# A cross-attention kernel: the hand-written order of its first two batches drawn anew

## The chip, the cores and the metric

The kernel runs on one core of one Trainium2 chip. The metric is the device time of one execution in microseconds (us); less is better. Engines: PE (TensorE, matmuls; PEld is its weight load), DVE (VectorE), ACT (ScalarE), POOL (GpSimd) and SP (SyncE, which here only issues DMAs). "POOLq" and "SPq" are the queues in which POOL and SP issue DMAs. Each engine works through its own instructions in program order and waits, in place, for what an instruction needs.

## The reference

x is 32 batches of 512 rows by 640 columns, the context 32 batches of 77 rows by 1024 columns, all in float32. The context has 77 rows, which is the length of its text part, so the object, other and ip parts are empty; what is left to compute is one attention over 77 keys with 20 heads of 32 columns:

```python
q = _heads(hidden_states @ to_q_w)
h_txt = _sdpa(q, _heads(ehs_txt @ to_k_w), _heads(ehs_txt @ to_v_w))
out = _merge(h_txt)
out = out @ to_out_w + to_out_b
out = (out + residual) / RESCALE
```

The softmax runs over the 77 keys, the scale is 1/sqrt(32), the residual is x, RESCALE is 1.

## The kernel before

**Number format.** Each float32 operand is split into a high part (a copy rounded to fp32r) and a low part (the difference). A product is three matmuls: high by high, high by low, low by high. So each "step" of products below is three PE instructions, the high part of anything is a copy on ACT, and the low part is a subtraction on DVE or POOL.

**First stage: keys and values of the context.** The context of all batches is 2464 rows, worked in groups of 512, the fifth and last of 416. For each group the rows are transposed in eight chunks k (DVE, tile craw), split (tile ct, ACT and DVE), and multiplied by the key and the value weights, giving five column blocks j of 128 each. Keys are split (tile ks) and stored in k_dram; values are transposed (DVE, tile vs), split and stored in v_dram. This part, up to about 200 us, is not touched by the change: it covers the first groups, and the keys of the fourth.

**Second stage: attention.** Per batch there are five column blocks (four heads each). For one block n: queries (five steps over k, tile pq, one PSUM bank), high copy and low parts with copies across halves (tile qt); scores in four row tiles t (tile sc, three PSUM banks); a row maximum (DVE, nm); exponentials with their sums (ACT, tile pn, four instructions per row tile); a reciprocal (DVE, rs) and normalisation (POOL); a blockwise transpose (DVE, one tile z); four stores of z to DRAM (tile pd); and, four blocks later (LAG = 4), two loads back (tile raw), split into tile pp (ACT, DVE, POOL), six value passes (PE, tile pa, one buffer), the sum of two halves (ACT copy aw, two adds on DVE), and the split into tile at. When all five blocks of a batch are there, the output projection (tile po, with wo_s) adds up in steps, bias and residual are added (tile xr) and the rows stored. x of the next batch is loaded, transposed and split meanwhile (tiles xs, xt).

**The order.** Nothing is scheduled by the compiler: three tables of tokens are worked through one by one, and each token issues one small piece. FILL covers the end of the first stage together with batches 0 and 1; PLAN one batch, repeated for 29 batches; LAST_ the last batch. A token's place in the table sets the order on the engine that runs it, and the order of buffer allocations; between engines only data and buffers set the time.

**How a token is read.** "Y" tokens (function special) belong to the first stage or to set-up; j is a column block, k a chunk, i a quarter:
- YVjk: value products of the fourth group (PE); Ytj, Yhj, Ylj: its transpose (DVE), high (ACT) and low part (DVE); Ysji: its stores (SP).
- Yrk, Yfk, Ydk: transpose (DVE), high (ACT) and low part (DVE) of chunk k of the last group's context.
- YJjk: key products of the last group (PE); YIj, Yij, Yoj: high (ACT), low (DVE), store (SP).
- YCjk: value products of the last group (PE); YTj, YHj, YLj: transpose (DVE), high (ACT), low (DVE); YDji: stores (POOL's queue).
- Yzi, Yai, YUc, Yuc: x of batch 0, loaded (POOL's queue), transposed (DVE), high (ACT) and low part (POOL); Yxi: x of batch 1 loaded (SP).
- Yqk, YQ, Yg, Yc: the first block's queries; Yk: its keys loaded (SP); Ym, Yn, Yp: clearing of tiles (POOL); Ywj: output weights of block j loaded into wo_s (SP); Yb: bias.

Other tokens have a batch letter, a block and an operation (function issue): "a" is the batch of the table's start, "b" the one behind it, and a block number 0 to 4. So a3s0 is row tile 0 of the scores of batch 0, block 3. Operations: q queries of the next block, Q its high part (ACT), k copies across halves (POOL), g low parts (DVE); s scores (PE), m maximum (DVE), e exponentials (ACT); r, N, z reciprocal (DVE), normalisation (POOL) and transpose into z (DVE) of the block before; w its stores (SP); d loads of raw (SP); c casts into pp (ACT), l and R its low parts (POOL, DVE); v value passes (PE); A copy of the lower half (ACT), a adds of the halves (DVE); h and L high and low part of at for the block before (ACT, DVE); p projection steps (PE), f adds (DVE), o stores, b bias (POOL), ur residual loaded; T, X, x transposes, high and low parts of x (DVE, ACT, POOL), ux loads of x, uk and uv loads of keys and values (SP), K copies of keys (POOL).

Buffers that matter for the change: ct has 9 buffers, so a chunk of the last group takes the place of one whose five value products are done; vs has two (j even and odd), so a transpose waits for the stores of the one before it; z and pa have one each; b2L, for instance, is the last reader of the pa tile that b2v0 and b2v1 write again.

Of the kernel before, what the change touches and what calls it, by code (L numbers as in the profile page):

```python
# [51 lines left out]
def kernel(  # L52
# [732 lines left out]
    def low_query(n, w):  # L785
# [1 line left out]
        nc.vector.tensor_tensor(qt[rows, 1 + w, :], pqs[n][rows], qt[rows, 0, :].bitcast(F32), ALU.subtract)  # L787

    FILL = (
# [43 lines left out]
    ).split()  # L833

    PLAN = (
# [292 lines left out]
```

## Time and profile before

| | us |
|---|---|
| median of 3 runs | 1865.92 |
| lowest, highest | 1861.2, 1865.97 |
| the profiled execution | 1860.52 |
| its span, first to last instruction | 1858.7 |

The page gives busy times by engine, then views of stretches, of one engine's timeline and of waits. In a row of a timeline the columns are start and duration (us), engine, line of the code, operation, output<-input, shape, and the number of instructions merged into it; in square brackets stands the idle time of the engine just before, and what ended it. A row of a stretch has its bounds and length, then busy time and count of PE, PEld, DVE, ACT and POOL, the granted clock, and the DMA engines' share and GB/s. Line numbers: L204 key and value products of the context, L542 queries, L577 scores, L602 exponentials, L694 value passes, L750 projection, L171/L179/L183 the context's transpose and split, L256/L262/L266 the same for values, L588 maximum, L617 normalisation, L624 the transpose into z, L633 the stores of z, L712 the adds of halves, L726/L731 the split into at, L672 the low part of pp, L1037 the output weights.

### The profile page before, as it was taken

Reading aid. Unit: us, or ns where it says so; the run is one execution under the profiler, and the core shown is the slowest. Engines: PE = TensorE matmul, PEld = TensorE weight load, DVE = VectorE, ACT = ScalarE, POOL = GpSimd, SP = SyncE. Lnnn points to the kernel's source line nnn. Section 1 sums busy time; section 2 is a strip of 40 time slices with the busy share of each in tenths; the row PEclk is TensorE's granted clock in tenths of the full one; section 3 lists DMA queues with packets and bytes.
Section 4 is the critical chain, followed back from the end, with each engine's and each line's share of the span. In section 5 each row is a group of like instructions: output and inputs, shape, how many; then the busy total and the mean of one; then the engine's idle time right before and its main releaser. Section 6 shows DMA issues by size and latency. Waiting matters only on the chain.

```text
span 1858.7 us, 37494 instructions
## 1 busy us (share of the span) xinstructions
PE 1843.8 (99%) x10332; PEld 1656.9 (89%) x10332; DVE 1563.8 (84%) x2502; ACT 1524.9 (82%) x6218; POOL 1301.7 (70%) x1120
## 2 busy tenths in 40 slices
PE   9999999999999999999999999999999999999999
PEld 7888897889999999999999999999999999999998
DVE  5444458899999999999999999999999999999996
ACT  3232248999999999999999999999999999999984
POOL 1100158787887787777778777887788878877874
PEclk9999999999999999999999999999999999999999
DMA  9879779889898888989988989899899988888875
GB/s 186 197 196 251 179 189 261 248 244 243 238 243 242 238 239 227 246 236 232 247 236 240 240 239 242 234 236 245 231 236 247 242 239 240 232 236 240 237 219 192
DMA packets 563295, 431.37 MB, mean 232 GB/s; under 512 B 191120, under 2 KB 471120, under 8 KB 563088
## 3 DMA queue, kind: packets, MB, share of 16 engines
q1 hardware_dynamic: 558192, 413.16, 84.6%
q0 software_dynamic: 4800, 15.65, 2.6%
q8 instruction: 85, 1.39, 0.3%
q14 instruction: 122, 1.00, 0.2%
q10 hardware_dynamic: 96, 0.16, 0.0%
HBM read 247.17 MB, written 181.64 MB: 231 GB/s over the span
## 4 chain that ended last, share of the span: by engine, by line
PE 93%; ACT 2%; DMA 1%; DVE 1%; SPq 1%; issue 1%; POOL 0%; DVEq 0%; ACTq 0%; POOLq 0%
PE po L750 30%; PE pq L542 28%; PE pa L694 12%; PE sc L577 11%; PE pk L204 6%; PE pv L204 6%; ACT pn L602 1%; DMA pd<-z 1%; SPq L531 0%; SPq L633 0%; DVE z L624 0%; POOL xt L320 0%; DMA v_dram<-vs 0%; DVE pp L672 0%; DMA cs<-in_ctx_dram 0%
## 5 line engine op out<-in xcount | busy, mean ns | idle before, releaser
L602 ACT ACTIVATE pn<-sc,nm 128x77 f32<-128x77 f32 x2560 | 795.8, 342 | 39.5 <-DVE nm L588 33.1
L750 PE MATMUL po<-wo_s,at 128*128 128x320 f32 x3840 | 708.1, 311 | 0.1
L750 PEld LDWEIGHTS po<-wo_s,at 128*128 128x128 f32 x3840 | 620.1, 189 | 41.5 <-DVE xr L765 0.6
L542 PE MATMUL pq<-xt,wq_s 128*128 128x512 f32 x2400 | 597.5, 394 | 1.1 <-DVE qt L787 0.8
L602 ACT ACTIVATION_READ_ACCUMULATOR pn<-sc,nm 128x1 f32 x2560 | 567.2, 222 | 0.0
L542 PEld LDWEIGHTS pq<-xt,wq_s 128*128 128x128 f32 x2400 | 436.6, 188 | 80.9 <-ACT pn L602 1.2
L617 POOL TENSOR_TENSOR pn<-pn,rs 128x1232 f32<-128x1232 f32 x160 | 388.0, 2425 | 91.2 <-DVE rs L612 87.5
L694 PE MATMUL pa<-pp,vb 128*128 128x512 f32 x960 | 341.6, 404 | 3.7 <-DVE at L731 2.0
L577 PEld LDWEIGHTS sc<-kb,qt 128*128 128x128 f32 x1920 | 303.9, 188 | 16.6 <-ACT pn L602 2.3
L588 DVE TENSOR_REDUCE nm<-sc 128x4 f32<-128x308 f32 x640 | 295.2, 466 | 23.0 <-PE sc L577 18.9
L577 PE MATMUL sc<-kb,qt 128*128 128x154 f32 (+1 forms) x1920 | 302.7, 274 | 2.7 <-ACT pn L602 1.9
L783 POOL CAST qt<-qt 64x512 fp32r<-64x512 f32 x320 | 196.8, 615 | 142.2 <-ACT qt L779 127.3
L712 DVE TENSOR_TENSOR pa<-pa,aw 64x512 f32<-64x512 f32 x320 | 222.1, 694 | 50.1 <-ACT aw L708 42.7
L624 DVE STREAM_TRANSPOSE z<-pn 128x1280 f32<-128x1280 f32 x160 | 241.1, 1507 | 14.1 <-DMA pd<-z 8.1
L679 POOL TENSOR_TENSOR pp<-raw,pp 64x512 fp32r<-64x512 f32 x160 | 206.7, 1292 | 64.7 <-ACT pp L661 56.1
L708 ACT COPY aw<-pa 64x1024 f32<-64x1024 f32 x160 | 162.1, 1013 | 88.4 <-PE pa L694 87.5
L787 DVE TENSOR_TENSOR qt<-pq,qt 64x512 fp32r<-64x512 f32 x320 | 216.6, 677 | 6.0 <-ACT qt L779 1.1
L320 POOL TENSOR_TENSOR xt<-xs,xt 128x512 fp32r<-128x512 f32 x160 | 203.6, 1300 | 20.0 <-ACT xt L316 15.2
L743 POOL TENSOR_TENSOR xr<-xr,bias 128x640 f32<-128x640 f32 x128 | 202.6, 1584 | 14.2 <-DMA xr<-in_x_dram 3.9
L672 DVE TENSOR_TENSOR pp<-raw,pp 128x1024 fp32r<-128x1024 f32 x160 | 196.2, 1226 | 0.0
L694 PEld LDWEIGHTS pa<-pp,vb 128*128 128x128 f32 x960 | 174.0, 189 | 14.9 <-ACT pp L663 2.8
L663 ACT CAST pp<-raw 128x1024 fp32r<-128x1024 f32 x160 | 168.5, 1053 | 1.0 <-DMA raw<-pd 1.0
(46 smaller groups left out, 1584.8 us busy)
## 6 DMA issues: line engine op xcount, KB each, us to landing
pd<-z SPq DMA_DIRECT2D x640, 160.0 KB, 3.3
raw<-pd SPq DMA_DIRECT2D x160, 512.0 KB, 4.5
xr<-in_x_dram SPq DMA_DIRECT2D x128, 320.0 KB, 3.8
out_dram<-xr SPq DMA_DIRECT2D x127, 320.0 KB, 3.7
xs<-in_x_dram SPq DMA_DIRECT2D x124, 320.0 KB, 5.9
raw<-pd SPq DMA_DIRECT2D x160, 128.0 KB, 4.1
v_dram<-vs SPq DMA_DIRECT2D x80, 192.0 KB, 4.1
k_dram<-ks POOLq DMA_DIRECT2D x20, 512.0 KB, 4.3
```

Source lines behind the costliest of these rows:

```text
L204: nc.tensor.matmul(held[j][:, :gn], w[:, k, a, :], cts[g, k][:, c, :gn], start=(k == 0 and n == 0), stop=(k == NK - 1 and n == 2),)
L542: nc.tensor.matmul(pqs[n], wq_s[:, k, a, j * P : (j + 1) * P], xts[b, k][:, c, :], start=(k == 0 and m == 0), stop=(k == NC_ - 1 and m == 2),)
L577: nc.tensor.matmul(sc[:, cols], qt[:, m, t * P : (t + 1) * P], keys_, start=(m == 0), stop=(m == 2),)
L588: nc.vector.tensor_reduce(nm, sc[:, :KCOLS].rearrange("p (h k) -> p h k", k=NKEY), AX.X, ALU.max, negate=True)
L602: nc.scalar.activation(pnb[n % 2][:, at, :NKEY], sc[:, i * NKEY : (i + 1) * NKEY], AF.Exp, bias=nm[:, i : i + 1], accum_out=sms[n][:, at : ...
L617: nc.gpsimd.tensor_tensor(pf, pf, rs.unsqueeze(2).to_broadcast([P, NQ * HPC, NKEY]), ALU.mult)
L624: nc.vector.transpose(z.rearrange("p b t j -> p t b j"), pn.rearrange("p (t h) k -> p t (h k)", t=NQ).rearrange("p t (b i) -> p t b i", i=Q),)
L679: nc.gpsimd.tensor_tensor(pp[64:, 4, :], raw[:64, 2, :], pp[:64, 4, :].bitcast(F32), ALU.subtract)
L694: nc.tensor.matmul(pas[n][:, p, :], vb[:, p, t, :], pp[:, c, :], start=(c == p), stop=(c == p + 2),)
L712: nc.vector.tensor_tensor(pa[64 * p : 64 * p + 64, 0], pa[:64, p], aw[:, p], ALU.add)
L750: nc.tensor.matmul(pos[b, t, h][:, :HALF], ats[b * NC_ + j][:, a, t * P : (t + 1) * P], wos[0][:, j, c, h * HALF : (h + 1) * HALF], start= ...
L787: nc.vector.tensor_tensor(qt[rows, 1 + w, :], pqs[n][rows], qt[rows, 0, :].bitcast(F32), ALU.subtract)
```

## The change

Only the table FILL is changed. It has the same 809 tokens before and after, each once; 37 of them stand at the same place. PLAN and LAST_ and all functions stay. By groups:
- the value products of the fourth group (YV) come in another order: YV20 to YV22 and YV40 sooner, YV11 to YV13 and YV31 later;
- the first transposes on DVE: Yt0 is now ahead of Yr0, and the transposes of x (Ya) are ahead of Yr3 and Yr4;
- the last group's keys: block 0 and 1 are taken first (YJ00 to YJ07 within the first 13 key steps), blocks 3 and 4 later, so the last ones (YJ33 to YJ37, YJ43 to YJ47) stand behind the first value step of that group, YC00, and behind queries a0q0 to a0q2;
- loads of keys, values, x and output weights (Yk, uk, uv, ux, Yw) and the stores of z (w) stand in another order on SP;
- in batches 0 and 1, steps of DVE, ACT and POOL change places by some positions; YL2 goes from behind a4N to block 3, YL4 from ahead of b0m0 to behind b0r; b1z and b2z go ahead of b1a0 and b2a0; b2L goes behind b2R.

The core of the diff:

```diff
--- before.py
+++ after.py
@@ -787,49 +787,49 @@
     FILL = (
 ...
-        "YV00 YV10 YV20 YV11 YV30 YV31 YV01 YV12 YV02 YV13 YV32 YV03 YV04 YV05 YV14 Yr0 YV06 Yf0 Yz1 Yd0 "
-        "YV07 Yz2 YV15 Yt0 YV40 Yz0 Yr1 Yz3 YV21 Yr2 Yf1 YV41 Yh0 YV42 Yf2 YV33 Yd2 Yr3 YV22 Yl0 YV23 "
-        "Yf3 Yd1 Ys00 YV16 Yr4 Ys01 YV24 Ya1 Ys02 YV43 Ya2 YV34 Ys03 Yf4 Yd3 YV35 Yr5 Yd4 YV25 Ya3 YV17 "
-        "YV44 Yt1 YV26 Ya0 Yf5 YV36 YU0 YV27 Yh1 YV45 YU1 Yt2 YV46 YU2 Yd5 YU3 Yl1 YV37 Yu2 Yr6 Yh2 Ys11 "
-        "YV47 Yf6 Yl2 Ys13 Yu1 Yr7 Ys10 Yd6 Yf7 Ys21 Ys22 Ys23 Ys12 Yt3 Yd7 YU4 Yu4 Yu3 Yu0 Yx0 Ys20 Yx2 "
-        "Yx1 Yh3 Yn0 Yt4 YJ00 YJ01 YJ20 YJ21 YJ10 YJ02 YJ22 YJ30 YJ11 YJ03 YJ12 YJ13 YJ23 YJ14 YJ24 YJ15 "
-        "YJ04 YJ05 YJ06 YJ16 YJ25 YJ31 YJ07 YJ32 YI0 YJ17 Yi0 Yq0 Yl3 YI1 Yo0 Yh4 YJ26 Yi1 YJ40 Yl4 Yo1 "
 ...
-        "Yk011 YJ47 YI3 a0K00 YC00 Yi3 YI4 a0K01 a0q0 Yi4 Yo3 a0q1 Yo4 Yn1 YC01 Ys40 Ym0 a0s0 a0q2 Ys42 "
 ...
-        "a3uk030 a1K10 a2q4 a3uk011 YD11 YC20 a2w1 a2Q YD10 a2w2 YC21 a2e3 a2g1 a2w0 a1K11 YC22 a2k0 "
-        "a2w3 YC23 a3r a2g0 a3uk020 YC24 a3N a3uk001 YC25 a3uk010 YC26 YC27 a3q0 a2x1 a3q1 a3z a3X2 a3q2 "
-        "a2k1 a3X3 a3s0 a3x2 a3X4 a3q3 a3m0 YT2 a3d0 a3d1 a4d1 a3w1 a3w3 a3e0 a3s1 a3x3 a3q4 a3w0 a3m1 "
 ...
-        "YC33 a4c0 a3g1 a4v1 a3e2 a4v0 a3k1 a3s3 a4q0 a3m3 a4l a3e3 a4s0 a4s1 a4m0 YC34 b0d0 a4K00 YH2 "
-        "a4v2 a4r b0ux3 a4s2 a4e0 a4N YL2 a4v3 a4ux1 a4q1 a4q2 a4v5 a4s3 a4K01 a4v4 b0uk111 YC41 a4m1 "
 ...
-        "b0v1 YD33 b1T1 b0q2 YH4 b0s1 YL4 b0q3 b0m0 YD40 b2T3 b0e0 b0v0 b0q4 YD42 b0r b1T2 YD41 b0v2 b0Q "
 ...
-        "b1Q b1v0 Yw0 b1m2 b1e0 b1v3 b1v2 Yb b1g1 b1v5 b1v4 b1s3 b1k1 b1g0 b1A b1k0 b1m3 b2q0 b2d1 b2c1 "
-        "b1a1 b2x1 b2q1 b1a0 b2c0 b2q2 b1z b2h b2l b2s0 b1e3 b2q3 b2L b2q4 b1w1 b1e2 b2m0 b1w2 b2v1 b2R "
-        "b2v0 b1w3 b2s1 b2Q b2v2 b2uv00 b2v3 b2e0 b2m1 b2k1 b2v5 b1w0 b2r b3p0 b2g0 b2d0 b2N b2v4 b2s2 "
-        "b2g1 b2A b2uv05 b2s3 b3uk011 b2m2 b3q0 b3c0 b2uv01 b2m3 b2a0 b2e1 b3q1 b2uv02 b2k0 b2a1 b3q2 "
-        "b3d1 b1K10 b2e2 b2uv06 b2z b2b0 b3s0 b3uk031 b3q3 b3h b3q4 b3L b3l Yw3 b3c1 b3p1 b3m0 b2w1 b3p4 "
 ...
-        "b3g1 b2w2 b3v3 b3v5 b3uk001 b3N b3X2 b3s2 b3m1 b3uk010 b3p6 b3X3 b3m2 b4q0 Yw4 b3A b3uk020 b3p7 "
 ...
-        "b3uk030 b4s0 b4h b3p3 b4c1 b4l b4q4 b4L b3w2 b3e2 b4d0 b4m0 b4v1 b4R b4d1 b4Q b4p9 b3w1 b4e0 "
 ...
 ...
+        "YV00 YV10 YV20 YV21 YV22 YV01 YV23 YV30 YV40 YV02 YV41 YV03 YV24 YV04 YV11 Yz3 YV42 Yz1 YV05 "
+        "Yz0 YV06 Yz2 YV07 YV43 Yt0 YV25 Yr0 YV44 Yf0 YV26 Yd0 Yr1 YV12 Yf1 YV31 Yh0 YV13 Yl0 YV32 Yd1 "
+        "Ys02 Yr2 YV14 Ys01 Yf2 YV33 Ys00 Yd2 YV45 Ya1 Ys03 YV15 Yr3 YV46 Yr4 Yf3 Ya3 YV16 YV27 Ya0 YV34 "
 ...
+        "YU1 Yd5 YU2 Ys13 Yu1 Yf6 Yr7 Ys12 Yd6 Yf7 Ys22 YU3 Yu2 Yd7 YU4 Ys11 Yu4 Ys23 Ys20 Yu3 Yt3 Yx0 "
+        "Yn0 Yh3 Yt4 YJ00 YJ01 YJ02 YJ10 YJ11 YJ03 YJ20 YJ04 YJ12 YJ05 YJ21 YJ06 YJ07 YJ22 YJ30 YJ23 "
 ...
+        "YJ42 Yi2 YJ31 Yl4 Yo2 Yq1 Yx1 Yx3 Yq2 Yq3 YJ32 YJ43 Yk000 Yq4 Yk030 Yk010 YC00 YQ Yk021 YJ44 "
 ...
+        "Yk031 YJ36 Yk011 a2T3 a0q1 a0K01 Ys30 YJ37 a0K00 a2X0 Ys43 a0q2 YI3 YJ47 Yi3 a0q3 Yo3 YI4 a0q4 "
 ...
+        "a2q0 YH1 a2m1 a2uv07 a2q1 YL1 a2e1 a2s2 YD12 a2q2 a2m2 YD10 a2e2 a2s3 a2q3 YD11 a3uk030 a2m3 "
+        "a2z a3uk011 YC20 a2X1 a1K11 a3uk021 a2q4 YD13 a2e3 a3uk031 a2x1 YC21 a2w2 a2Q YC22 a2w1 a2e0 "
+        "YC23 a3uk000 a2g0 a2k0 YC24 a2w3 a2k1 a2w0 YC25 a3r a2g1 b1uv16 a3N YC26 a3uk020 YC27 a3s0 a3q0 "
 ...
+        "a3x3 a3q3 a3X4 a4d1 YC31 YH2 a3w0 a3x4 YC32 a4c0 YL2 a3w3 a3q4 a4c1 a4ux1 a3s2 a4K01 a3m1 YC40 "
 ...
+        "a4R YC35 a3e3 YD20 a4q0 b0d1 a4v2 a4v5 a4r a4v4 a4N a4s0 a4A a4s1 a4m0 a4q1 a4m1 b0c1 a4a0 a4s2 "
 ...
+        "b0m0 YH4 YD30 b0q2 b0m1 b0e0 b0r YL4 b0s2 b0N b2T3 b0q3 b1d0 b0e1 b0v1 b1T2 b1d1 b0v3 b0q4 b0T0 "
 ...
+        "b1v2 b1v5 Yw1 b1Q b1v4 b1s3 b2X1 b2uv01 b1g1 Yb b1A b1m3 b1g0 b1k1 b2c0 b1k0 b1a1 b1e3 b2q0 b2l "
+        "b1z b2c1 b2q1 b1a0 b1e2 b1w1 b2s0 b2uv00 b0uk110 b2h b2q2 b2m0 b1w2 b2R b2e0 b2s1 b1ur0 b2q3 "
+        "b1w0 b2r b0uk100 b2L b2q4 b2N b2uv03 b2m1 b2s2 b2Q b1w3 b2v1 b2m2 b2v0 b2e1 b2d0 b2v3 b2g1 b2v2 "
 ...
+        "b2k0 b3d0 b3X2 b3uk030 b2a1 b3q2 b2e3 b3x2 b2z b3q3 b3q4 b3X3 b1K10 b3X4 b2a0 b2b0 b2w0 b3s0 "
 ...
+        "b3s3 b3A b3uk020 b4q0 b3m3 b3x3 b2uv06 b4q1 Yw4 b3e3 b3a1 b3ur1 b4q2 b3a0 b3k1 b3uk001 b4q3 "
 ...
+        "b4v0 b4R b4v1 b4d0 b4p9 b3w3 b4p8 b4e0 b4v3 b3uk021 b4g0 b4b1 b4v2 b3w2 b4g1 b4s2 b4ux0 b4v4 "
 ...
     ).split()
```

46 rows, old and new, of the table FILL are left out of this document.

## The prediction

> **What bounds the kernel now.** I read first the page's busy shares, then the table of stretches, then TensorE's timeline for the places where it stands still, and last the rows of the engines that end those waits.
>
> ```profile
> span 1858.7 us, 37494 instructions
> PE 1843.8 (99%) x10332; PEld 1656.9 (89%) x10332; DVE 1563.8 (84%) x2502; ACT 1524.9 (82%) x6218; POOL 1301.7 (70%) x1120
> ```
>
> TensorE is busy 99% of the span, so only its idle time can be won, and only work that makes it idle can be lost.
>
> ```profile
> 200.00:250.00 50.00, 49.70 (x236) 43.58 (x235) 23.16 (x37) 13.24 (x25) 14.05 (x15) 1.00 0.72 186
> 250.00:300.00 50.00, 49.30 (x263) 45.24 (x262) 32.64 (x50) 32.94 (x156) 40.01 (x43) 1.00 0.82 198
> 300.00:350.00 50.00, 44.71 (x229) 37.12 (x229) 45.03 (x73) 45.91 (x198) 41.46 (x41) 1.00 0.88 262
> 350.00:392.00 42.00, 41.29 (x242) 37.16 (x241) 38.50 (x60) 38.40 (x165) 31.41 (x28) 1.00 0.90 251
> 392.00:441.00 49.00, 49.00 (x286) 44.61 (x285) 44.67 (x72) 45.06 (x191) 39.18 (x34) 1.00 0.89 241
> ```
>
> Columns are the stretch, then busy time of PE, PEld, DVE, ACT and POOL. FILL runs from 200 to about 355 us. TensorE idles 0.3 + 0.7 + 5.3 + 0.7 = 7.0 us up to 392, and not at all in the batch after it (49.00 of 49.00): from there on it is the bound, so a delay that FILL leaves stays in the end, one for one, and so does a gain. Here are the places:
>
> ```profile
> 228.09 14.24 PE L204 MATMUL pk<-ct,wk_s 128*128 128x416 f32 x75 [0.21 <-ACT xt L316]
> ...
> 286.29 0.34 PE L577 MATMUL sc<-kb,qt 128*128 128x154 f32 x1 [0.69 <-POOL qt L783]
> ...
> 312.77 0.73 PE L577 MATMUL sc<-kb,qt 128*128 128x308 f32 x3 [1.90 <-ACT pn L602]
> 318.25 0.47 PE L694 MATMUL pa<-pp,vb 128*128 128x512 f32 x1 [0.89 <-DVE at L731]
> 321.37 2.31 PE L542 MATMUL pq<-xt,wq_s 128*128 128x512 f32 x9 [0.81 <-DVE qt L787]
> 325.64 0.70 PE L694 MATMUL pa<-pp,vb 128*128 128x512 f32 x2 [0.20 <-DVE at L731]
> 341.26 0.73 PE L542 MATMUL pq<-xt,wq_s 128*128 128x512 f32 x2 [0.21 <-POOL xt L320]
> 344.66 0.47 PE L694 MATMUL pa<-pp,vb 128*128 128x512 f32 x1 [1.16 <-ACT pp L663]
> ```
>
> In order these are YJ00, a3s0, b1s0, b1v1, b2q0, b2v1, b4q3 and b4v1. Their waits add up to 6.1 us. Between 300 and 350 ACT (45.9 of 50) and VectorE (45.0) are nearly full, and the waits end on them.
>
> **The change, part by part.** The table holds the same 809 steps in another order, so no instruction is added or removed: every cost is a wait that goes, comes or changes place. The sum is made against the profiled execution's own 1860.5 us (span 1858.7 and 1.8 around it).
>
> *First part, to the last keys.* VectorE now starts with Yt0, and its transposes of x (Ya) stand ahead of Yr3 and Yr4. TensorE takes YJ07 after 12 other J steps instead of 22. By the row at 228.09 a step is 3 x 14.24/75 = 0.57 us, so it is reached at 228.1 + 12 x 0.57 = 234.9, about 5.7 us sooner.
>
> ```profile
> 222.10 1.57 DVE L306 STREAM_TRANSPOSE xs<-xs 128x640 f32<-128x640 f32 x2 [3.38 <-DMA xs<-in_x_dram]
> ...
> 227.86 0.55 DVE L183 TENSOR_TENSOR ct<-craw,ct 128x416 fp32r<-128x416 f32 x1
> 228.55 0.69 DVE L266 TENSOR_TENSOR vs<-vs 128x512 fp32r<-128x512 f32 x1
> 229.16 0.60 DVE L171 STREAM_TRANSPOSE craw<-cs 128x416 f32<-128x416 f32 x1
> ...
> 231.93 1.16 DVE L183 TENSOR_TENSOR ct<-craw,ct 128x416 fp32r<-128x416 f32 x1
> ```
>
> Yd7 must be done by then. Behind the landing of x (222.1) VectorE has four Ya (0.78), five Yr (0.55 to 0.60), five Yd (0.55), two Yt and two Yl (0.69 each as the upper row): 3.1 + 2.8 + 2.8 + 2.8 = 11.5 us, so Yd7 ends at 233.6 with no hindrance, and at 234.8 if the last two Yd take 1.16 us as the one at 231.93 did while POOL worked on xt. The cover is between 1.3 and 0.1 us; what is missing of it TensorE would lose at YJ06 and YJ07. I take +0.3 here, bounds -0.2 (YJ00's wait goes) and +1.8 (three slow ones). Drawing nine J steps behind YC00, and three query steps ahead of YJ47, costs TensorE nothing: it has other steps of the table in their place, and what is late next, YI3 and YI4, only feeds stores on SP.
>
> *Second part, batch 0.* The 0.69 us at a3s0 go: POOL did a3N and a2x1 ahead of a2k1, the copy that a3s0 needs.
>
> ```profile
> 284.28 1.29 POOL L320 TENSOR_TENSOR xt<-xs,xt 128x512 fp32r<-128x512 f32 x1
> 285.63 0.61 POOL L783 CAST qt<-qt 64x512 fp32r<-64x512 f32 x1
> ```
>
> In the new table a2k1 stands ahead of a3N. In exchange three query steps move behind a3s0, which is neutral. On SP a3uk030 to a3uk031 now come ahead of a2w2. They overwrite keys that a2s3 still reads, and the stores of a2 wait behind them; but a1w was issued sooner, and I find a2w ending where it ended before. I cost it at 0; without that cover it is the four issues, about 2 us by the rows of SP below, which a3z would feel.
>
> *Third part, where the time is.* ACT is full from b0e0 on, and b0e0 waited for VectorE:
>
> ```profile
> 308.51 0.33 ACT L602 ACTIVATE pn<-sc,nm 128x77 f32<-128x77 f32 x1 [1.11 <-DVE nm L588]
> ```
>
> ```profile
> 294.76 2.69 DVE L266 TENSOR_TENSOR vs<-vs 128x416 fp32r<-128x416 f32 x1 [0.17 <-ACT vs L262]
> ...
> 303.54 0.58 DVE L266 TENSOR_TENSOR vs<-vs 128x416 fp32r<-128x416 f32 x1
> ...
> 307.44 0.59 DVE L266 TENSOR_TENSOR vs<-vs 128x416 fp32r<-128x416 f32 x1
> ```
>
> Between a4m0 and b0m0 VectorE loses YL2 (2.69 us, moved ahead to a3) and YL4 (0.59, moved behind b0m0), 3.3 us. TensorE gives a4s0 about 1.4 us later (2.1 us of products more ahead of it, less the 0.69), and a4g1 will wait some 0.7 us for a4Q. So b0m0 comes 1.2 us sooner; bounds 0 and 1.9. That lead is spent again: up to b1g0 VectorE has YL4 (0.59) and b1m3 (0.46 by the row at 325.43 below) more to do, so b2q0, which needs b1g0, starts 0.15 us sooner. It is the point where the sum is taken anew, since VectorE and not TensorE sets it; b1s0's and b1v1's waits lie ahead of it and may change size freely (b1q0 to b1q2 now come ahead of b1s0, and wait for b0g0 instead).
>
> ```profile
> 322.08 1.42 DVE L712 TENSOR_TENSOR pa<-pa,aw 64x512 f32<-64x512 f32 x2 [0.48 <-ACT aw L708]
> 323.43 1.49 DVE L624 STREAM_TRANSPOSE z<-pn 128x1280 f32<-128x1280 f32 x1
> 324.85 0.64 DVE L731 TENSOR_TENSOR at<-pa,at 128x512 fp32r<-128x512 f32 x1
> 325.43 0.45 DVE L588 TENSOR_REDUCE nm<-sc 128x4 f32<-128x308 f32 x1
> 325.81 1.20 DVE L672 TENSOR_TENSOR pp<-raw,pp 128x1024 fp32r<-128x1024 f32 x1
> 326.94 0.46 DVE L588 TENSOR_REDUCE nm<-sc 128x4 f32<-128x308 f32 x1
> 327.33 0.23 DVE L612 RECIPROCAL rs<-sm 128x16 f32<-128x16 f32 x1
> ```
>
> These rows are b1a1 with b1a0, b1z, b2L, b2m0, b2R, b2m1, b2r. The only pa tile is free for b2v0 when b2L is done. The new order is b1a1, b1z, b1a0, b2m0, b2R, b2r, b2L: 0.45 + 1.20 + 0.23 = 1.9 us more ahead of b2L, which then ends near 327.3. TensorE has two score steps more ahead (0.7) and would be there at 326.1: it waits 1.2 instead of 0.20, that is +1.0. Behind it the 0.21 at b4q3 is covered, and at b4v1 TensorE comes 0.6 us later for its larger queue (b4s1, b4v0) and 0.6 for the delay, so that the 1.16 vanish nearly whole: -1.16 + 0.0. Sum from b2q0 on: -0.15 + 1.0 - 0.21 - 1.1 = -0.5.
>
> *Output weights.* Yw2, Yw0, Yw1 move within a few issues; Yw3 comes sooner. Yw4 has five other loads ahead of it on SP that it had not, and three fewer: two issues, about 1.0 us by the rows of SP below.
>
> ```profile
> 340.41 0.43 SPq L1037 DMA_DIRECT2D wo_s<-wo_dram x1
> ```
>
> It landed in time for b4p9, the step right behind b4v1. Bounds 0 (it still lands in time) and +1.4 (that 1.0 with the 0.43 of its own issue); I take +0.3, nearer to the first since b4p9 also comes later. **The sum:** -0.5 + 0.3 = -0.2 us; the +0.3 of the first part lies ahead of b2q0 and is inside its lead. So 1860.5 becomes 1860.3. The runs shown are 1861.2, 1865.92 and 1865.97, and with the profiled one that makes two near 1861 and two near 1866. I put the base in the middle of 1860.5 and the median, 1863.2, and predict 1863.0.
>
> **A rule against it.** The row at 294.76 is 2.1 us longer than its like at 303.54, and POOL's a4N ran beside it. The Trainium skill (SBUF — State Buffer, Who interferes with whom) says that a VectorE instruction with two SBUF inputs and a GpSimd instruction that reads SBUF lock each other out, whichever starts second waiting for the whole of the first. This trace agrees there. By that rule YL4, now between b0r and b2T3 just as b0r releases b0N, could be the one that waits, and the sum would be +1.9 instead of -0.2.
>
> **The rivals.**
>
> *YL4 is caught as YL2 was* (b0N wins by a hair): +2.1 us on VectorE ahead of b1g0, so b2q0 and all behind it: 1863.0 + 2.1 = 1865.1. Against it: YL4 is next in VectorE's own queue, and b0N must hear of b0r first.
>
> *x lands late.* Yr3 to Yd7 stand behind x now, where Yr3 and Yr4 were ahead. Each microsecond beyond 222.1 is lost at YJ03 to YJ07; 3 us gives 1866.
>
> *Slower: z holds VectorE.* One mechanism, at b1z, b2z and b3z: the transpose overwrites z, so it needs the four stores of the one before landed, and VectorE queues behind it.
>
> ```profile
> 324.94 1.36 SPq L633 DMA_DIRECT2D pd<-z  x3
> 326.35 0.51 SPq L531 DMA_DIRECT2D vb<-v_dram  x1
> 326.91 0.48 SPq L633 DMA_DIRECT2D pd<-z  x1
> ...
> 342.36 1.51 DVE L624 STREAM_TRANSPOSE z<-pn 128x1280 f32<-128x1280 f32 x1 [1.64 <-DMA pd<-z]
> ```
>
> The last row shows that such a wait is real (b3z). The four b1w were spread over 5 issues of 2.45/5 = 0.49 us; now they lie among 9, so the last comes 2.0 us later, and b1a0 and b2a0 wait behind their z (1.5 each), and with them b2h, b3h and the pa tile. If all reaches TensorE: the lost lead 0.9, b2L 1.0, stores 2.0, the two add-halves 3.0 = +6.9, so 1870.1. It decides from 0.5 us more than the room that I find at b3v1, where two more steps on TensorE give it some 2 us.
>
> *Faster: the waits just go.* If the order fits as drawn, all 6.1 us of the rows above vanish: 1863.2 - 6.1 = 1857.1. For it: the stretch 300 to 350 has 5.3 us of idle, and ACT's work is the same. Against it: ACT and VectorE at 90% leave no room to take it all.
>
> **Numbers.** Likeliest 0.32 (its own range 1859 to 1868), YL4 0.07, late x 0.07, z 0.31, waits go 0.23. A change of 0.3%, 5.6 us, is about what a measurement of this kernel can tell. Faster: 0.23 and 0.04 from the likeliest's low end, 0.27. Slower: 0.31 and 0.04, 0.35. Same: the rest, 0.38. Range: 1856, below which only a gain beyond the waits lies, to 1874, the z case on the upper base (1865.9 + 6.9 = 1872.8) with 1.4 for Yw4's bound.
>
> **What would show it.** Right: no wait at a3s0; b0e0 near 307.3; a wait near 1.2 us on VectorE at b2v1; none or little at b4v1; the batch from b = 3 on still 49.0 us. Wrong: TensorE idle at YJ05 to YJ07; VectorE waiting for pd<-z at b1z or b2z by more than 1 us; PE idle in 200 to 392 under 3 us or over 10; any change of the 49.0, since the sum rests on a steady state that FILL can't touch.

## The result, and the profile after

| | before | after |
|---|---|---|
| median of 19 runs each, us | 1862.47 | 1859.58 |
| lowest and highest, us | 1858.69, 1866.63 | 1857.15, 1862.78 |
| profiled execution, us | 1860.52 | 1858.27 |

The ratio is 0.9985 (95% interval 0.9979 to 0.9992): 2.8 us faster, from 1.5 to 3.9. It is a real gain, but under the 5.6 us that the prediction set as its bound, so by its own measure the outcome is "same". 1863.0 was predicted, 3.4 us too high. In a later comparison two of 12 runs of the changed kernel took 6373 and 2203 us, for reasons that no trace shows; they are left out wherever its times are compared.

The page of the changed kernel and its stretches, with the columns of before:

```profile
span 1856.5 us, 37492 instructions
PE 1842.4 (99%) x10332; PEld 1655.7 (89%) x10332; DVE 1563.4 (84%) x2502; ACT 1527.2 (82%) x6218; POOL 1303.9 (70%) x1120
```

```profile
200.00:250.00 50.00, 50.00 (x241) 44.78 (x240) 25.07 (x39) 13.29 (x25) 15.73 (x16) 1.00 0.72 186
250.00:300.00 50.00, 50.00 (x269) 45.94 (x268) 34.39 (x57) 37.27 (x177) 40.03 (x44) 1.00 0.85 207
300.00:350.00 50.00, 44.86 (x230) 37.14 (x229) 43.63 (x70) 45.53 (x192) 41.34 (x39) 1.00 0.93 265
350.00:392.00 42.00, 40.76 (x237) 36.62 (x236) 38.66 (x61) 38.04 (x163) 31.98 (x27) 1.00 0.89 232
392.00:441.00 49.00, 49.00 (x286) 44.56 (x286) 44.66 (x72) 45.02 (x189) 39.13 (x34) 1.00 0.88 243
```

TensorE does not idle between 200 and 300 any more (1.0 us before), idles 5.1 us between 300 and 350 (5.3 before) and 1.2 up to 392 (0.7 before). A batch is 49.00 us as before. Its waits, from its timeline:

```profile
308.50 2.31 PE L542 MATMUL pq<-xt,wq_s 128*128 128x512 f32 x9 [0.94 <-DVE qt L787]
313.45 0.59 PE L577 MATMUL sc<-kb,qt 128*128 128x308 f32 x3 [0.90 <-ACT pn L602]
318.43 1.62 PE L542 MATMUL pq<-xt,wq_s 128*128 128x512 f32 x6 [1.94 <-ACT pp L661]
323.41 1.20 PE L694 MATMUL pa<-pp,vb 128*128 128x512 f32 x4 [0.23 <-DVE at L731]
333.93 1.80 PE L694 MATMUL pa<-pp,vb 128*128 128x512 f32 x5 [0.83 <-DVE at L731]
```

These are b1q0, b1s2, b2q0, b2v1 and b3v1. The waits at YJ00, a3s0, b4q3 and b4v1 are gone, and those at b1s0, b1v1 and b2q0 (1.90 + 0.89 + 0.81 = 3.60 us) have become those at b1q0, b1s2 and b2q0 (0.94 + 0.90 + 1.94 = 3.78). The span has no zero that both kernels share, because the 200 us ahead of the table vary: YV00 starts at 200.5 and 198.6 us in two traces of before. So from here on times are counted from the first product of YV00, and F is the time from there to the first query of batch 5 (counted from 0), by which everything that FILL does is settled. Where the later expectations give batch 5 some 145 us, they mean the token b5q0, near the end of the table.

| from YV00, us | before, two traces | after, three traces |
|---|---|---|
| b0m0 | 107.43, 107.03 | 103.86, 103.74, 103.99 |
| b2q0 | 120.85, 120.51 | 119.36, 119.24, 119.49 |
| b4v1 | 144.14, 143.34 | 142.75, 142.64, 142.90 |
| F | 289.27, 288.06 | 287.90, 286.29, 286.71 |

Up to b2q0 an order repeats within 0.4 us; F varies by 1.6 in itself. Its mean falls from 288.67 to 286.97: 1.7 us. The 26 batches behind F take 1273.8 to 1274.2 us in every trace of this study. The lead is 3.4 us at b0m0 and 1.3 at b2q0, and about that much stays: 1.4 at b5q0 (147.53 and 146.78 before, 145.59, 145.72 and 145.95 after).

### The profile page after: what moved, and what is told of

Same layout as the page of the kernel before. It is cut to its first block, busy times and chain, and to the rows that moved or that the text cites. A ratio compares the mean times of both kernels' runs of the same rounds, so it can differ in the third digit from the quotient of the medians.

```text
span 1856.5 us, 37492 instructions
## 1 busy us (share of the span) xinstructions
PE 1842.4 (99%) x10332; PEld 1655.7 (89%) x10332; DVE 1563.4 (84%) x2502; ACT 1527.2 (82%) x6218; POOL 1303.9 (70%) x1120
## 4 chain that ended last, share of the span: by engine, by line
PE 93%; DMA 4%; SPq 1%; DVE 1%; ACT 1%; issue 0%; POOL 0%; DVEq 0%; ACTq 0%; POOLq 0%
PE po L750 29%; PE pq L542 28%; PE pa L694 12%; PE sc L577 11%; PE pv L204 7%; PE pk L204 6%; DMA pd<-z 1%; DMA cs<-in_ctx_dram 1%; DMA xr<-in_x_dram 1%; DMA wo_s<-wo_dram 0%; DMA wraw<-in_L_xattn_to_v_w_dram 0%; DMA xs<-in_x_dram 0%; DMA wraw<-in_L_xattn_to_k_w_dram 0%; ACT pn L602 0%; DMA raw<-pd 0%
## 5 line engine op out<-in xcount | busy, mean ns | idle before, releaser
L708 ACT COPY aw<-pa 64x1024 f32<-64x1024 f32 x160 | 162.2, 1014 | 85.0 <-PE pa L694 83.9
```

## Where the lead is won and lost: first runs

Where VectorE and ScalarE stand still in the changed kernel, by their timelines:

```profile
285.37 1.42 DVE L266 TENSOR_TENSOR vs<-vs 128x416 fp32r<-128x416 f32 x1 [0.86 <-ACT vs L262]
...
296.49 0.69 DVE L787 TENSOR_TENSOR qt<-pq,qt 64x512 fp32r<-64x512 f32 x1 [0.60 <-ACT qt L779]
...
297.94 0.62 DVE L256 STREAM_TRANSPOSE vs<-pv 128x416 f32<-128x416 f32 x1
...
303.83 0.52 DVE L266 TENSOR_TENSOR vs<-vs 128x416 fp32r<-128x416 f32 x1
...
316.36 0.69 DVE L787 TENSOR_TENSOR qt<-pq,qt 64x512 fp32r<-64x512 f32 x1 [1.22 <-ACT qt L779]
317.09 0.48 DVE L588 TENSOR_REDUCE nm<-sc 128x4 f32<-128x308 f32 x1
317.60 0.68 DVE L787 TENSOR_TENSOR qt<-pq,qt 64x512 fp32r<-64x512 f32 x1
```

```profile
303.03 0.54 ACT L262 CAST vs<-vs 128x416 fp32r<-128x416 f32 x1 [1.95 <-DVE vs L256]
...
306.34 0.59 ACT L779 CAST qt<-pq 128x512 fp32r<-128x512 f32 x1 [0.31 <-PE pq L542]
307.32 1.01 ACT L708 COPY aw<-pa 64x1024 f32<-64x1024 f32 x1 [0.39 <-PE pa L694]
```

The first rows are YL2 at its new place, a4g1 (0.60 for a4Q), YT3, YL4, b1g1, b1m3 and b1g0. Between a4m0 and b0m0 the work of VectorE falls from 14.15 to 10.57 us (the busy times of its instructions added up), because YL2, YL4 and a4r (0.25) have left that stretch, and its idle time there is 0.8 us instead of 1.0. ScalarE is idle 1.95 us ahead of YH4 and b0e0, and then 0.7 more (0.31 and 0.39). The 1.94 at b2q0 carry the name of another engine, but b1g0 ends at 317.60 + 0.68 = 318.28 and b2q0 starts right behind: it is b1g0, as the prediction said of before. b1g0 stands behind b1g1, that behind b1Q, that behind b1q4, which TensorE does behind b1s2 and its 0.90.

Theory after the result: the whole rearrangement of VectorE's queue around a4 gives the lead, and the new order's own idle time on ScalarE takes most of it back ahead of b2q0. Rivals: YL2's place alone gives it; the 0.69 at a3s0 are a part of it; b2L's place takes it back, as predicted. Two controls and two orders with one edit each came first.

**Controls.** 

> The kernel before once more, as a control. Let F be the time from the first product of YV00 to the first query product of batch 5; it was 289.3 us before and 287.9 in the changed kernel, and what lies ahead of YV00 took 200.5 and 199.1. If F belongs to the table, it comes back as 289.3 within 0.3, whatever the part ahead of YV00 takes. If F scatters by a microsecond or more by itself, its 1.4 us of difference say nothing.

> The changed kernel once more, as a control: F back at 287.9 within 0.3 if F belongs to the table; anywhere between 287 and 290 if it scatters.

Measured: 1857.28 and 1858.49 (a second run of before beside them: 1862.51). Up to b2q0 they repeat within 0.4 us; F does not (288.06 instead of 289.27, 286.29 instead of 287.90). A single time of this kernel tells nothing about 2 us, which is why the following runs are read by the trace.

**b2L back ahead of b2m0 and b2R; b1z and b2z back behind the add-halves.**

```diff
-b1z b2c1 b2q1 b1a0 ... b2h b2q2 b2m0 b1w2 b2R b2e0 ... b2r b0uk100 b2L
+b2c1 b2q1 b1a0 b1z ... b2h b2L b2q2 b2m0 b1w2 b2R b2e0 ... b2r b0uk100
-b2z b3q3 b3q4 b3X3 b1K10 b3X4 b2a0
+b3q3 b3q4 b3X3 b1K10 b3X4 b2a0 b2z
```

> The changed kernel with three places of VectorE as before: b2L ahead of b2m0 and b2R, b1a0 ahead of b1z, b2a0 ahead of b2z. The prediction's step (b2L late, so TensorE waits 1.0 more at b2v1): b2L about 1.5 us sooner, F about 287. The rival, that ScalarE is full from b0e0 on and sets the end whatever VectorE's order is there: F stays at 287.9 within 0.4, since b2L can't run ahead of b2h on ScalarE.

Measured: 1860.51, F 289.70, later than any trace of the changed kernel and than either expectation. VectorE and ScalarE of that run:

```profile
322.25 0.62 ACT L726 CAST at<-pa 128x512 fp32r<-128x512 f32 x1
324.06 0.33 ACT L602 ACTIVATE pn<-sc,nm 128x77 f32<-128x77 f32 x1 [1.20 <-DVE nm L588]
```

```profile
322.90 0.69 DVE L731 TENSOR_TENSOR at<-pa,at 128x512 fp32r<-128x512 f32 x1 [1.29 <-ACT at L726]
```

b2L has to wait for b2h, which ScalarE does late in the new order. Put ahead of b2m0 it stops VectorE for 1.29 us, b2e0 waits 1.20 for b2m0, and b3q0 starts at 128.8 from YV00 instead of 127.1 to 127.4. (Another 1.7 us of F go with a piece at half clock further on, on which the last section tells more; the same holds for what comes behind b2q0 with YL2 back, below.) So b2L behind b2R and b2r is not a loss but fits b2h's new place: those 1.9 us of VectorE's work are done while b2L could not run.

**YL2 back behind a4N.**

```diff
-YC32 a4c0 YL2 a3w3 ... YC35 a3e3 YD20 a4q0 ... a4v4 a4N a4s0
+YC32 a4c0 a3w3 ... YC35 a3e3 a4q0 ... a4v4 a4N YL2 YD20 a4s0
```

> The changed kernel with YL2 back behind a4N, where it took 2.69 us before. Lead theory (VectorE's chain from a4m0 sets b0e0, and b0e0 sets the end): YL2 near 2.7 us, b0m0 and b0e0 2 to 2.7 us later than in the changed kernel, F up by 1.5 to 2.5. Rival (the lead of b0e0 is spent again up to b2q0, as the prediction had it): b0e0 just as late, but F up by less than 0.5.

Measured: 1859.52. Both expectations had YL2 at 2.7 us; it lasts 0.53, because it starts 0.23 us ahead of a4N. b0m0 comes at 104.58 instead of 103.9, b2q0 at 119.68, within the 0.4 by which orders repeat. YL2's place by itself is not what gives 3.4 us in the new order; what a YL2 of 2.69 us would cost there was not seen.

**The same move alone in the old order**, together with YH2:

```diff
-a3m0 YT2 a3d0 a3d1 a4d1 a3w1 a3w3 a3e0 a3s1 a3x3 a3q4 a3w0 a3m1
+a3m0 YT2 a3d0 a3d1 a4d1 a3w1 a3w3 a3e0 YH2 a3s1 a3x3 a3q4 a3w0 a3m1 YL2
-YC34 b0d0 a4K00 YH2 a4v2 ... a4N YL2 a4v3
+YC34 b0d0 a4K00 a4v2 ... a4N a4v3
```

> The order of before with two steps moved: YH2 behind a3e0 and YL2 behind a3m1, away from a4N. Times are counted from the first product of YV00. Theory (YL2, held 2.69 us beside a4N between a4m0 and b0m0, is what the change takes out of VectorE's queue): YL2 lasts near 0.55, b0m0 falls from 107.0-107.4 to 104-105, as in the changed kernel. If that one move makes the gain, b2q0 falls from 120.5-120.85 to 119.5 or less. Rival (b0m0 is held by something else, the scores or ScalarE): YL2 is short but b0m0 stays above 106 and b2q0 above 120.4. Second rival (the lead needs the rest of the new order): b0m0 comes sooner, b2q0 doesn't.

Measured: 1860.55 (before beside it 1860.11); b0m0 at 108.34 and b2q0 at 123.96, later than before, the second in part by a piece at half clock at 315.1. YL2 lasts 1.57 us at its new place, beside a low part of x on POOL, and not 0.55; the times are those of the first rival. VectorE of that run:

```profile
288.39 1.57 DVE L266 TENSOR_TENSOR vs<-vs 128x416 fp32r<-128x416 f32 x1 [0.78 <-ACT vs L262]
...
297.46 1.51 DVE L624 STREAM_TRANSPOSE z<-pn 128x1280 f32<-128x1280 f32 x1 [1.26 <-POOL pn L617]
...
302.97 0.62 DVE L256 STREAM_TRANSPOSE vs<-pv 128x416 f32<-128x416 f32 x1 [0.95 <-PE pv L204]
```

The rows are YL2, a4z and YT3. VectorE waits for YH2 with a3g0 behind it; and with YL2 gone from its old place, a4z waits for a4N and YT3 for the products of YC3. YL2's 2.69 us had filled time in which VectorE would have waited anyway: from a4m0 to b0m0 it is 14.03 us instead of 14.38 in the profile of before, and 10.6 in the changed kernel. VectorE's work there falls by 2.7 us, and its idle time rises from 1.0 to 3.2. The changed kernel has no wait at YT3 (297.94 above), where YC35 stands ahead of a4q0, and a4r ahead of a4m0, so that POOL starts a4N sooner. That these two together make the 3.4 us is read from the traces; each was not undone by itself.

**a2x1 and a2k1 back behind a3N in the new order.**

```diff
-a3uk031 a2x1 YC21 ... YC24 a2w3 a2k1 a2w0 YC25 a3r a2g1 b1uv16 a3N YC26
+a3uk031 YC21 ... YC24 a2w3 a2w0 YC25 a3r a2g1 b1uv16 a3N a2x1 a2k1 YC26
```

> The changed order with a2x1 and a2k1 back behind a3N, which brings the wait at a3s0 back. Theory: TensorE waits some 0.7 us at a3s0 (81.5 becomes 82.2 from YV00), but the copies behind it are not what sets b0m0, so b0m0 stays within 0.3 of 103.8 and b2q0 within 0.4 of 119.3: the 0.69 us that went there is no part of the gain. Rival (TensorE's own order carries it): b0m0 and b2q0 both come 0.7 later, 104.5 and 120.0.

Measured: 1862.05, with b0m0 at 108.14 and b2q0 at 123.65. Both expectations were too small. TensorE's timeline, and its stretches there:

```profile
283.22 0.34 PE L577 MATMUL sc<-kb,qt 128*128 128x154 f32 x1 [2.76 <-POOL qt L783]
```

```profile
280.50:283.90 3.40, 0.68 (x3) 0.60 (x4) 0.30 (x1) 0.00 (x0) 2.60 (x3) 1.00 0.84 242
283.90:287.30 3.40, 3.40 (x12) 3.02 (x11) 2.18 (x3) 2.27 (x10) 2.17 (x2) 0.54 0.78 236
```

The new order reaches a3s0 2.4 to 3.2 us sooner (81.5 from YV00, 83.9 and 84.7 before), mostly because a3q0 to a3q2 now stand behind it, so the same place of a2k1 costs 2.76 us there and not 0.69. And behind it the granted clock is 0.54: TensorE is busy throughout and starts 12 matmuls, at half the clock, another 1.7 us (half of 3.41). 2.76 + 1.7 = 4.5, and a4s0 is 4.1 to 4.4 us later than in the three traces of the changed kernel. The lead at b0m0 needs a2k1's new place: with the 1.7 us of the clock taken off, the run still loses 2.6 of its 3.4.

## Can more be won?

**The queries of b1 sooner.** The chain b1q4, b1Q, b1g1, b1g0 pulled forward:

```diff
-b1q3 b1m1 ... b1e0 b1r b1s2 ... b1v1 b1q4 b1e1 b0uk111 b1m2 ... Yw1 b1Q b1v4 ... b1g1 Yb b1A b1m3 b1g0
+b1q3 b1q4 b1m1 ... b1e0 b1Q b1r b1s2 ... b1v1 b1e1 b0uk111 b1m2 b1g1 b1g0 ... Yw1 b1v4 ... Yb b1A b1m3
```

> The changed order with the queries of b1 finished sooner: b1q4 ahead of b1s2, b1Q ahead of b1e1, b1g1 and b1g0 ahead of b1m3. Theory (the 1.94 us of TensorE's wait at b2q0 hang on the chain b1q4, b1Q, b1g1, b1g0, since b1q4 stands behind b1s2, which waits 0.90 for b0e3): b2q0 comes 1.0 to 1.8 us sooner than 119.3 from YV00; what it leaves in batch 5 is less, 0 to 1.5 us, because ScalarE has no room to follow. Rival (VectorE's work in that stretch, not the chain, sets b2q0): b2q0 stays within 0.4 of 119.3.

Measured: 1855.8 (before beside it 1860.11); b2q0 at 117.37, 1.9 sooner, b3q0 0.2 to 0.5 sooner, b5q0 at 145.35 instead of 145.6 to 146.0, F 286.46. TensorE's waits:

```profile
312.72 0.60 PE L577 MATMUL sc<-kb,qt 128*128 128x308 f32 x3 [0.21 <-ACT pn L602]
315.97 1.60 PE L542 MATMUL pq<-xt,wq_s 128*128 128x512 f32 x6 [0.82 <-DVE qt L787]
...
322.46 1.20 PE L694 MATMUL pa<-pp,vb 128*128 128x512 f32 x4 [0.61 <-DVE at L731]
333.37 1.64 PE L694 MATMUL pa<-pp,vb 128*128 128x512 f32 x5 [1.01 <-DVE at L731]
```

The 1.94 and 0.90 have become 0.82 and 0.21, and most of the gain is spent up to b2v1, which waits for b2L and so for b2h and comes only 0.4 to 0.6 us sooner: ScalarE has no idle time in between.

**ScalarE's idle time drawn together.** The core of the edit:

```diff
-YC45 a4e3 b0uk130 b1T1 YD33 YC46 a4w3 b0R b0q0 YD32 b0s0 YC47 ... YT4 b0q1 b0m0 YH4 YD30 b0q2 b0m1 b0e0 b0r YL4 b0s2 b0N b2T3
+YC45 b0s0 b0s1 a4e3 b0uk130 b1T1 b0m0 b0m1 b0e0 b0e1 YD33 YC46 a4w3 b0R b0q0 YD32 YC47 b0s2 ... YT4 b0m2 YH4 b0e2 YL4 b0r b0N b0T0
```

> The changed order with its idle time on ScalarE drawn together. b0s0 and b0s1 ahead of YC46, b0m0 and b0m1 ahead of b0R, so that b0e0 follows a4e3 without the 2.0 us of idle time; b0e2 and b0e3 brought up to fill the gaps of 0.4 at b0Q and b0A; b1q4, b1Q, b1g1, b1g0 as in the run with the queries sooner; the transposes b2T3 and b1T2 behind b2g0. Theory (from b0m0 on ScalarE and VectorE set the time, and what is idle there can be won): b0e0 2 us sooner than 104.3 from YV00, b2q0 2 to 3.2 sooner than 119.3, and 1.5 to 3 us of it left at batch 5; the time near 1856.5. Rival (the lead is spent again behind b2q0, as after the change): b2q0 sooner, but the first query of batch 5 within 0.7 of 145.6, and the time unchanged near 1859.

Measured: 1861.26. b0e0 comes at 102.2, 2 us sooner as expected; b2q0 at 119.83, not sooner. TensorE and POOL of that run:

```profile
313.36 1.32 PE L577 MATMUL sc<-kb,qt 128*128 128x154 f32 x5 [1.91 <-POOL qt L783]
```

```profile
306.11 2.27 POOL L617 TENSOR_TENSOR pn<-pn,rs 128x1232 f32<-128x1232 f32 x1 [3.08 <-DVE rs L612]
308.33 2.58 POOL L271 DMA_DIRECT2D v_dram<-vs  x4
310.96 0.61 POOL L783 CAST qt<-qt 64x512 fp32r<-64x512 f32 x1
```

b0N came later, and behind it POOL issues four stores (2.58 us) before the copy b0k1, for which b1s0 waits. A piece at half clock begins right behind that wait, at 313.46, and may have a part in the late b2q0. In the next edit the copies stand ahead of the stores:

```diff
-YD31 YT4 ... YL4 b0r b0N b0T0 b0q1 YD30 ... YD41 b0v5 b0v4 b0g1 YD40 b0A b0g0 b0z YD42 b1c1 b0k1
+YD31 YD30 YT4 ... YL4 b0r b0N b0T0 b0q1 ... b0v5 b0v4 b0g1 b0k1 b0k0 YD41 YD40 YD42 YD43 b0A b0g0 b0z b1c1
```

> The run with ScalarE's idle time drawn together, mended: there POOL issued four stores of the last group's values (2.58 us) ahead of the copy b0k1, which b1s0 waited for (1.91 us on TensorE). Now b0k1 and b0k0 stand ahead of YD40 to YD43, YD30 ahead of b0N, b2x0 behind b1k0, and b2d0 and b2d1 ahead of b1w. Theory (those stores took the lead): b1s0 without a wait of over 0.3, b2q0 near 117 from YV00 instead of 119.8, b3v1 below 134, batch 5 begins 1 to 2 us sooner than 145.4, and no granted clock below 1 between 200 and 392 us. Rival (POOL is short of time here, and what is taken from one wait comes back in another): b2q0 above 118.5, or batch 5 not sooner than 145.4.

Measured: 1859.07. b1s0 has no wait and no piece of FILL runs at half clock, b2q0 comes at 117.71, but b3v1 at 135.87 and b5q0 at 147.37, so the rival held. b0e0 is at 102.55, 1.6 us sooner than with the queries alone (104.16), and b2q0 is no sooner than there (117.37): ScalarE's idle time ahead of b0e0 is not what holds b2q0 once the queries are sooner. VectorE now runs from b0m0 to b2L almost without a gap, and TensorE waits 1.26 for it at b2v1 and more behind:

```profile
323.84 1.19 PE L694 MATMUL pa<-pp,vb 128*128 128x512 f32 x4 [1.26 <-DVE at L731]
331.54 0.60 PE L577 MATMUL sc<-kb,qt 128*128 128x308 f32 x3 [1.17 <-POOL kb L519]
335.90 0.70 PE L694 MATMUL pa<-pp,vb 128*128 128x512 f32 x2 [1.28 <-DVE at L731]
```

**The loads b2d0 and b2d1 sooner**, on top of the queries sooner. They move from behind b2e1 and b2s3 to behind Yb, ahead of b1w1 to b1w3 on SP.

> The order with the queries of b1 sooner, and the loads b2d0 and b2d1 brought from behind b2e1 to ahead of the stores b1w on SP. In the run before, ScalarE stood 0.88 us at b3c0 for these rows, and TensorE 1.01 us at b3v1 behind it. Theory (the wait at b3v1 is that load's, since b3Q, b3h and b3c1 queue behind b3c0): the gap at b3c0 goes, the wait at b3v1 falls to 0.3 or less, b3v1 comes 0.7 sooner than 134.8 from YV00 and batch 5 begins near 144.7 instead of 145.4; b2q0 stays at 117.4. Rival (b3v1's wait is held by something else, or the loads delay the stores b1w, and with them z at b2z): b3v1 unchanged or later, and VectorE waits for pd<-z at b2z.

Measured: 1860.76; the rival held. The gap at b3c0 went, but b3v1 came 0.8 us later and b5q0 3.7 later, 1.7 of it by a piece at half clock behind the last wait here:

```profile
330.35 1.51 DVE L624 STREAM_TRANSPOSE z<-pn 128x1280 f32<-128x1280 f32 x1 [1.99 <-DMA pd<-z]
```

```profile
334.72 1.16 PE L694 MATMUL pa<-pp,vb 128*128 128x512 f32 x4 [1.62 <-DVE at L731]
...
337.57 0.50 PE L694 MATMUL pa<-pp,vb 128*128 128x512 f32 x1 [1.70 <-DVE pp L672]
```

Two issues ahead of b1w hold VectorE 1.99 us at b2z (0.77 and nothing in the two traces with the queries sooner, nothing in the three of the changed kernel), and b2a0, b3h and b3L behind it. This is the prediction's slower rival, met in another order; the run with the copies first had these loads sooner too, and 2.30 us at b2z.

**The queries sooner, timed.** 

> The changed kernel once more, timed beside the one with the queries sooner. Expected: 0.9985 of before, as found, within its interval of 0.9979 to 0.9992; about 1859.5.

> The changed order with b1q4 ahead of b1s2, b1Q ahead of b1e1, and b1g1 and b1g0 ahead of b1m3, now timed. In its one look b2q0 came 1.9 us sooner, batch 5 only 0.3 sooner than after the change, and no window of 3.41 us held more than 1.2 us of idle TensorE, so that no granted clock fell in the part that the table covers. Theory (the wait removed at b2q0 is spent again behind it on ScalarE and VectorE, but TensorE's clock isn't lost any more in some executions): its median lies 0.3 to 1.5 us below the changed kernel's, near 1858.5, and its highest time is lower. Rival (the lead counts): 2 us below, near 1857.5. Second rival (nothing is left): equal within 0.3 us.

Measured on one chip: before 1861.24, the changed kernel 1858.35 (ten runs), ratio 0.9985 (0.9976 to 0.9994); with the queries sooner 1857.58, ratio 0.9982 (0.9973 to 0.9990), from 1856.24 to 1859.15. That is faster than before, and 0.8 us below the changed kernel, but the intervals overlap: between these two nothing is decided. One reading of the theory fell: the changed kernel's own times (1855.92 to 1859.17) are hardly more spread in this comparison.

## Why the prediction held, point by point

The time lay in the range, and "same" was the likeliest of its three answers. The steps did less well: two failed, the size of the lead at b0m0 and the wait at b2v1, and both erred to the same side, so that the forecast change is -0.2 us and the measured one -2.8. That the range holds both is owed to its width.

*What bounds the kernel*: right. 49.00 a batch, 1273.8 to 1274.2 us behind F in every order; only waits in FILL can be won.

*First part, +0.3 (bounds -0.2 to +1.8)*: it is the lower bound. YJ05 to YJ07 have no wait, and YJ00's 0.21 is gone.

*Batch 0, the 0.69 at a3s0*: gone, and the cover found for SP held. What the step did not see is that the three query steps moved behind a3s0, which it called neutral, had covered most of the wait for a2k1: without them its new place is worth 2.76 us there, and 1.7 more in the run that undid it.

*"So b0m0 comes 1.2 us sooner; bounds 0 and 1.9"*: the direction is right, the size is 3.4. The work that leaves VectorE's queue was priced nearly right, 3.3 us against 3.6 (a4r was left out). Of the two terms set against it, a4s0 comes 0.6 us later and not 1.4 (92.7 against 92.5 and 91.8), and the 0.7 foreseen at a4g1 are 0.60 but replace other waits, so that VectorE's idle time doesn't grow. And the reason given falls short: YL2 was taken off the queue as if the queue were full, but the run with YL2 moved in the old order shows waits in the same place instead. It takes the rest of the new order for its time to be won.

*"That lead is spent again", b2q0 0.15 sooner*: it is spent, 3.4 becomes 1.3. It was priced on VectorE by YL4 and b1m3 (1.05 us); the traces show the chain of b1q4 ahead of b2q0, and with that chain sooner b2q0 comes 1.9 us sooner. ScalarE's 1.95 us of idle time ahead of b0e0 lies on the way too, but the order that took most of it away as well brought b2q0 no further (117.71 instead of 117.37).

*"It waits 1.2 instead of 0.20, that is +1.0" at b2v1*: this step failed. The wait is 0.23. The prediction moved b2L on VectorE alone and did not look where b2h had gone on ScalarE; the run with b2L back shows that b2L cannot start sooner.

*b4q3 and b4v1, -0.21 and -1.1*: right; neither wait is in the changed kernel's timeline. *Yw4, +0.3*: b4p9 has no wait, the lower bound. At b3v1 a wait of 0.83 came that no step had.

*The sum*: -0.2 was predicted between profiled executions; F shows -1.7, and the runs -2.8. Replacing the +1.0 at b2v1 by 0, the 0.15 by 1.3, and the +0.3 of Yw4 by 0 gives -0.2 - 1.0 - 1.15 - 0.3 = -2.65, and with the 0.83 at b3v1 -1.8, near the -1.7 of F. The base of 1863.2 was sound: the median of before in 19 runs is 1862.47.

*The rivals*: YL4 was not caught (0.52 us at 303.83, b0N from 304.06), x was not late, z did not wait. YL2, whose cost at its new place the prediction left out, was caught there too: it lasts 1.42 us and ends 0.45 us behind the low part of x that POOL works on until 286.34; in the profile of before it ended 0.45 us behind a4N. "The waits just go" came true in part: of its 6.1 us, the waits at YJ00, a3s0, b4q3 and b4v1, 2.3 us, are gone, but 0.83 came at b3v1.

## What to carry to other kernels

Where an order written by hand is drawn anew, a step's cost is read on the engine that it waits for in the *new* order: b2L's place looked like a loss until b2h's was read beside it, and a2k1's old place costs four times as much once TensorE arrives sooner. Taking an instruction out of a queue wins its time only if the queue has no wait behind it: ask what its neighbour would wait for without it. And DMA issues count on the engine that makes them: four stores ahead of one copy, or two loads ahead of four stores, took back what two edits had won, though in two of these three runs a piece at half clock is in it too.

## What the runs showed of the hardware

TensorE's granted clock fell behind pieces of 3.41 us in which it stood still for little more than half. In the traces the granted clock is recorded in such pieces, on a grid that lies elsewhere in each execution, and is 1.0 or 0.5. Two cases, each a piece with a wait and the next one; the first is the run of before among the controls, the second the one with YL2 back. The rows lie up to 0.3 us beside the pieces, hence 0.54 and not 0.5; by the pieces themselves the idle time ahead is 1.97 and 1.93 us:

```profile
308.20:311.60 3.40, 1.22 (x8) 1.05 (x8) 3.31 (x6) 3.38 (x16) 3.25 (x5) 1.00 1.02 364
311.60:315.00 3.40, 3.40 (x11) 2.80 (x10) 3.11 (x6) 3.40 (x16) 3.17 (x4) 0.54 0.79 286
```

```profile
316.70:320.10 3.40, 1.47 (x9) 1.17 (x8) 2.61 (x5) 3.35 (x11) 3.13 (x4) 1.00 0.89 281
320.10:323.50 3.40, 3.40 (x12) 2.76 (x11) 3.29 (x4) 3.40 (x16) 0.70 (x1) 0.54 0.90 315
```

In the fourteen traces of this study, their last 20 us aside, every piece with 1.9 us or more of idle TensorE (by the modelled ends of its matmuls) was followed by one at half the clock, six of six; with 1.5 to 1.8 us it was 6 of 13, and below 1.5 us never. So a wait of 1.9 us costs no more than itself when the grid cuts it in two, as the 1.94 at b2q0 in the profile of the changed kernel (0.94 and 1.00), and up to 1.7 us more when it does not, as in the run with YL2 back. The Trainium skill (TensorE: Matmul & The Clock Gate, What's actually happening) describes a free-running window of about 3.4 us, which these traces confirm, and has the clock halved after an idle window; here a window that is idle for little more than half was enough. The slower piece need not cost its 1.7 us: in the second trace of before, whose piece lies behind b1s0, the waits behind it shrink (none at b1v1, 0.55 us at b2q0, instead of 0.89 and 0.81), and b2q0 comes no later, at 120.51 instead of 120.85.

This also bears on the spread of before. Each timed run lists its mean granted clock, which one such piece lowers by 0.5 x 3.41 / 1858 = 0.0009. Of the 23 runs of before in the last comparison, one at 0.949 aside, the 13 at 0.997 or 0.998 have a mean of 1861.75 us and the 9 at 0.999 or 1.0 one of 1860.02, a difference of 1.7 us. The ten runs of the changed kernel there and those with the queries sooner are all at 0.999 or 1.0. If that difference is the clock's, about 13/22 x 1.7 = 1.0 us of the measured gain goes with it and the rest with the order itself. That it is has not been shown: where in those timed runs the slow pieces lie was not seen, and the trace of before with such a piece in FILL is the quicker of the two (F 288.06 instead of 289.27). The three traces of the changed kernel have none in FILL.

Nor are such pieces what makes F vary by 1.6 us in the changed kernel. Up to b5q0 its three traces agree within 0.4 us; between b5q0 and F TensorE waits 1.25 us in the first (0.62, 0.23 and 0.40 at 352.64, 375.29 and 383.64, each time for VectorE's low part of at) and 0.05 and 0.06 us in the others. Why these waits come in one execution and not in the next stays open.
